# A two-layer graph kernel on one core: two splits moved among earlier units, one convolution kept back for the last batch, the verdict's product moved to the end

## The chip, the cores and the metric

The kernel runs on one core of one Trainium2 chip. The metric is the device time of one execution in microseconds (us); the kernel before takes 3221.36 us, the median of three executions (3220.45 to 3222.96). One core has five engines that run side by side and wait for each other through semaphores: TensorE (PE in the profile: matrix products, with PEld for its weight loads), VectorE (DVE), ScalarE (ACT), GpSimd (POOL) and SyncE (SP, which issues the transfers). Each engine has a queue of its own and works through it in program order.

## What is computed

The input `x` is 32 batches of 512 rows and 512 columns; `adj` is a 512 x 512 matrix of zeros and ones. There are two layers, each with a residual and a layer normalisation. The first is attention with 8 heads of 64 columns, restricted by `adj`; the second multiplies by `adj` from the left and by a weight from the right. Cut to what matters:

```python
def _L0_gnn_ref(x, adj, Wq, bq, Wk, bk, Wv, bv):
    q = (x @ Wq + bq).reshape(b, n, H, HD)          # k and v likewise
    scores = jnp.einsum('bihd,bjhd->bhij', q, k) / jnp.sqrt(jnp.float32(HD))
    scores = scores + jnp.where(adj == 0, -1e9, 0.0)[None, None, :, :]
    weights = jax.nn.softmax(scores, axis=-1)
    return jnp.einsum('bhij,bjhd->bihd', weights, v).reshape(b, n, H * HD)

def _L1_gnn_ref(x, adj, weight, bias):
    y = jnp.einsum('nm,bmd->bnd', adj, x)           # the aggregation
    return jnp.einsum('bnd,do->bno', y, weight) + bias   # the convolution

x = _layernorm(x + _L0_gnn_ref(x, adj, Wq, bq, Wk, bk, Wv, bv), axis=-1)
x = _layernorm(x + _L1_gnn_ref(x, adj, weight, bias), axis=-1)
```

All of it is float32. The kernel computes the first layer's softmax without subtracting a maximum, and ends in a verdict: if the sums of exponentials or the adjacency are out of the expected range, a general kernel computes everything again. With these inputs it isn't run.

## The kernel before

The kernel is scheduled by hand: the order in which the operations are written is the order in each engine's queue. The main loop goes through 32 batches `b` with 4 pairs of heads `hp` each. In every step it writes the scores of the next pair, the attention product of this pair, and then some filler for TensorE, taken from a list of units that belongs to the batch: the projections of batch b + 1 (7 products of a Strassen-Winograd scheme for each of q, k and v, so 21 units), the first layer's normalisation, the aggregation and the convolution of batch b - 1, and the transposes of x of batch b + 2. Each unit has a weight (a convolution unit 1.0, a projection 0.5, an aggregation product 0.55, a transpose unit 0.13, all else 0), and `work_until` takes units until the share of the pair is used up.

TensorE's products go to three PSUM tiles, named `bank`, in rotation; scores have two tiles `ps`, the attention product one, `po`.

```python
    def scores(b, hp, half):
        for j in (2 * half, 2 * half + 1):
            ps = psum.tile([P, 2, N], FP, name="ps", bufs=2)
            for s in range(2):
                ...
                nc.tensor.matmul(ps[:, s, :], keys[:, j * P:(j + 1) * P], queries, start=True, stop=True)
            e = E[b, hp, j] = work.tile([P, 2, N], FP, name="e", bufs=6)
            nc.scalar.activation(e, ps, AF.Exp, scale=1.0 / root)
            nc.vector.tensor_mul(e, e, edge[:, j, None, :].to_broadcast([P, 2, N]))   # the mask, L461
            if j == 1:
                ES[b, hp] = work.tile([P, 2, N], FP, name="es", bufs=3)
                nc.gpsimd.tensor_add(ES[b, hp], E[b, hp, 0], e)
            elif j > 1:
                nc.gpsimd.tensor_add(ES[b, hp], ES[b, hp], e)

    def project(b, which, i):       # one of seven products for q, k or v
        ...
        pm = bank(2, half)
        for r in range(2):
            for d in range(2):
                nc.tensor.matmul(pm[:, r, :], left[:, d, r * P:(r + 1) * P], right[:, d, :], ...)   # L338
        ...                         # then its eviction: on ScalarE for two units of q and k, else on VectorE

    def normalise(t, slot):
        row = X[t - slot // NB][:, slot % NB, :]
        nc.vector.tensor_scalar(row, row, STAT[t][:, slot, 0:1], RSTD[t][:, slot:slot + 1],
                                op0=ALU.subtract, op1=ALU.mult)

    def split(b, d):
        high = HIGH[b, d] = work.tile([P, NB, P], FR, name="high")
        low = LOW[b, d] = work.tile([P, NB, P], FR, name="low")
        cols = X[b][:, :, d * P:(d + 1) * P]
        nc.scalar.activation(high, cols, AF.Copy)
        nc.vector.tensor_sub(low, cols, high.bitcast(FP))

    def aggregate(b, d):
        if d == 0:
            YT[b] = work.tile([P, DB, N], FP, name="yT", bufs=1)
        pm = bank(N)
        parts = [part[:, m, :] for part in (LOW.pop((b, d)), HIGH.pop((b, d))) for m in range(NB)]
        for n, part in enumerate(parts):
            nc.tensor.matmul(pm, part, adjT[:, n % NB, :], start=(n == 0), stop=(n == 2 * NB - 1))
        nc.scalar.activation(YT[b][:, d, :], pm, AF.Copy)
        if d == DB - 1:
            for c in range(NB):
                nc.gpsimd.tensor_add(X[b][:, c, :], X[b][:, c, :], b1_r)

    def convolve(b, c):
        pm = bank(D)
        for d in range(DB):
            nc.tensor.matmul(pm, YT[b][:, d, c * P:(c + 1) * P], w1[:, d, :],
                             start=(d == 0), stop=(d == DB - 1))
        nc.vector.tensor_add(X[b][:, c, :], pm, X[b][:, c, :])
        statistics(b, 1, c)

    def aggregation(b):

        if b < 0:
            return []
        splits, products = ([(f, b, d) for d in range(DB)] for f in (split, aggregate))
        units = splits[:2]
        for d in range(DB):
            units += products[d:d + 1] + splits[d + 2:d + 3]
        return units

    def convolution(b):
        return [(convolve, b, c) for c in range(NB)] if b >= 0 else []
```

[...] ScalarE rounds 128 columns of x to `high`, VectorE subtracts to get `low`, and the aggregation multiplies both by the adjacency, `low` first. `high` and `low` have two buffers each.

The list of a batch's units, and the end of the kernel:

```python
            chores += [(normalise, b - 1, c) for c in range(NB)]
            chores = [(square_root, b - 1, slots), (invert_root, b - 1, slots)] + chores if b > 0 else []
            units = []
            for k, unit in enumerate(made[:-2]):
                units.append((unit, 0.5))
                if k > 0:
                    units += [(u, 0.0) for u in chores[:1]]
                    chores = chores[1:]
            units += [(u, 0.0) for u in chores]
            units += [(u, 0.55 if u[0] is aggregate else 0.0) for u in gathered[:5]]
            units += [(u, 0.5) for u in made[-2:]]
            for unit in gathered[5:]:
                units += [(u, 0.13) for u in turned[:1]] + [(unit, 0.55 if unit[0] is aggregate else 0.0)]
                turned = turned[1:]
            units += [(u, 0.13) for u in turned]
            if b < B - 1:
                units += [(u, 1.0) for u in convolved]
            begun = 0 if b < B - 1 else 1
            share = sum(w for _, w in units) / (HP - 2 * begun)
            done = 0.0
...
        def work_until(part):

            nonlocal done
            begin = share * (hp - begun) + (0.25 if hp % 2 else 0.0)
            end = share * (hp - begun + 1) + (0.0 if hp % 2 else 0.25)
            while units and (units[0][1] == 0 or done < begin + (end - begin) * part - 0.3):
                unit, w = units.pop(0)
                run([unit])
                done += w
...
    run([u for u, _ in units])
    t = B - 1
    rest, gather = convolution(t - 1), aggregation(t)
    run(rest[:2])
    invert(t, 1)
    residual(t, 2)
    residual(t, 3)
    square_root(t, slice(0, NB))
    invert_root(t, slice(0, NB))
    for c in range(NB):
        normalise(t, c)
    run(gather[:2] + rest[2:] + gather[2:])
    if t > 0:
        square_root(t, slice(NB, 2 * NB))
        invert_root(t, slice(NB, 2 * NB))
        for slot in range(NB, 2 * NB):
            normalise(t, slot)
        store(t - 1)
    judge()
    for c in range(NB):
        convolve(t, c)
        slot = NB + c
        square_root(t + 1, slice(slot, slot + 1))
        invert_root(t + 1, slice(slot, slot + 1))
        normalise(t + 1, slot)
        store(t, [c])
```

The list's order in a middle batch is thus: 19 projections, with the normalisations between them; split 0, split 1, product 0, split 2, product 1; the last 2 projections; a transpose unit, split 3, a transpose unit, product 2, a transpose unit, product 3, the last transpose unit; 4 convolution units. `judge()` makes the verdict's 128 flags with seven small VectorE operations, sums them with a one-column matmul, and compares the sum.

Of the kernel before, what the change touches and what calls it, by code (L numbers as in the profile page):

```python
# [39 lines left out]
ALU = mybir.AluOpType  # L40
# [4 lines left out]
P = 128  # L45
# [157 lines left out]
def fast_kernel(ctx: ExitStack, tc, verdict, x, adj, Wq, bq, Wk, bk, Wv, bv, W1, b1, out):  # L203
    nc = tc.nc
    B, N, D = x.shape
    H = Wq.shape[1] // HD
    HP = H // 2
    NB = N // P
    DB = D // P
# [8 lines left out]
    def bank(*shape):  # L218

        return psum.tile([P, *shape], FP, name="bank", tag="bank", bufs=3)  # L220
# [9 lines left out]
    def load_blocks(b):  # L230

        for c in range(NB):
            IN[b, c] = work.tile([P, D], FP, name="xin", bufs=NB)
            nc.sync.dma_start(IN[b, c], x[b, c * P:(c + 1) * P, :])
# [27 lines left out]
    ones = consts.tile([P, P // GROUP], FP, name="ones")  # L262
# [96 lines left out]
    def flips(b):  # L359
        return [(x_transpose, b, c) for c in range(NB)] if b < B else []  # L360

    def projections(b):


        if b >= B:
            return []
        units = [(project, b, which, i) for which in "qkv" for i in ORDER]
        for n in (5, 12):
            units[n:n + 4] = units[n + 2:n + 4] + units[n:n + 2]
        return units  # L370
# [14 lines left out]
    def square_root(t, slots):  # L385
        nc.scalar.activation(RSTD[t][:, slots], STAT[t][:, slots, 1], AF.Sqrt, bias=eps)  # L386

    def invert_root(t, slots):
        nc.vector.reciprocal(RSTD[t][:, slots], RSTD[t][:, slots])  # L389
# [5 lines that stand above are left out]
# [8 lines left out]
    def store(b, blocks=None):  # L403
        for c in blocks or ():
            nc.sync.dma_start(out[b, c * P:(c + 1) * P, :], X[b][:, c, :])
        if blocks is None:
            nc.sync.dma_start(out[b].rearrange("(c p) d -> p c d", p=P), X[b])
# [27 lines left out]

    def aggregation(b):

        if b < 0:
            return []
        splits, products = ([(f, b, d) for d in range(DB)] for f in (split, aggregate))  # L440
        units = splits[:2]
        for d in range(DB):
            units += products[d:d + 1] + splits[d + 2:d + 3]
        return units

    def convolution(b):
        return [(convolve, b, c) for c in range(NB)] if b >= 0 else []
# [4 lines left out]
# [4 lines that stand above are left out]
                lanes = slice(s * HD, (s + 1) * HD)  # L456
                keys, queries = KT[b][hp // 2][lanes, hp % 2, :], QT[b][hp // 2][lanes, hp % 2, :]
# [3 lines that stand above are left out]
            nc.vector.tensor_mul(e, e, edge[:, j, None, :].to_broadcast([P, 2, N]))  # L461
# [5 lines that stand above are left out]
# [52 lines left out]
    def judge():  # L519
        seen = consts.tile([P, 3], FP, name="seen")  # L520
        nc.vector.tensor_reduce(seen[:, 0:1], sums, axis=AX.X, op=ALU.add)
        nc.vector.tensor_reduce(seen[:, 1:2], inverses, axis=AX.XY, op=ALU.add)
        nc.vector.tensor_reduce(seen[:, 2:3], inexact, axis=AX.X, op=ALU.add)
        well = consts.tile([P, 3], FP, name="well")
        nc.vector.tensor_scalar(well[:, 0:2], seen[:, 0:2], BOUND, None, op0=ALU.is_le)
        nc.vector.tensor_scalar(well[:, 2:3], seen[:, 2:3], 0.0, None, op0=ALU.is_equal)
        nc.vector.tensor_mul(well[:, 0:1], well[:, 0:1], well[:, 1:2])
        nc.vector.tensor_mul(well[:, 0:1], well[:, 0:1], well[:, 2:3])
        pm = bank(N)
        nc.tensor.matmul(pm[0:1, 0:1], well[:, 0:1], ones[:, 0:1], start=True, stop=True)  # L530
        nc.vector.tensor_scalar(verdict, pm[0:1, 0:1], P - 0.5, None, op0=ALU.is_lt)


    def run(units):
        for unit in units:
            unit[0](*unit[1:])
# [3 lines left out]
    first = projections(0)  # L540
# [6 lines left out]
    combine(wv, bv_r)  # L547
    run(first[13:])

    pairs = [(b, hp) for b in range(B) for hp in range(HP)]  # L550
    scores(*pairs[0], 0)
    run(flips(1))
    scores(*pairs[0], 1)
    for i, (b, hp) in enumerate(pairs):
        if hp == 0:



            made, turned = projections(b + 1), flips(b + 2)
            gathered, convolved = aggregation(b - 1), convolution(b - 1)  # L560

            slots = slice(0, 2 * NB if b > 1 else NB)
            chores = [(normalise, b - 1, c) for c in [*range(NB, 2 * NB)] * (b > 1)] + [(turn_over, b)] * (b > 1)
            chores += [(normalise, b - 1, c) for c in range(NB)]
            chores = [(square_root, b - 1, slots), (invert_root, b - 1, slots)] + chores if b > 0 else []
            units = []
            for k, unit in enumerate(made[:-2]):
                units.append((unit, 0.5))
                if k > 0:
                    units += [(u, 0.0) for u in chores[:1]]  # L570
                    chores = chores[1:]
            units += [(u, 0.0) for u in chores]
            units += [(u, 0.55 if u[0] is aggregate else 0.0) for u in gathered[:5]]
            units += [(u, 0.5) for u in made[-2:]]
            for unit in gathered[5:]:
                units += [(u, 0.13) for u in turned[:1]] + [(unit, 0.55 if unit[0] is aggregate else 0.0)]
                turned = turned[1:]
            units += [(u, 0.13) for u in turned]
            if b < B - 1:
                units += [(u, 1.0) for u in convolved]  # L580
            begun = 0 if b < B - 1 else 1
            share = sum(w for _, w in units) / (HP - 2 * begun)
            done = 0.0
        if hp == 1 and b + 2 < B:
            load_blocks(b + 2)

        def work_until(part):

            nonlocal done
            begin = share * (hp - begun) + (0.25 if hp % 2 else 0.0)  # L590
            end = share * (hp - begun + 1) + (0.0 if hp % 2 else 0.25)
            while units and (units[0][1] == 0 or done < begin + (end - begin) * part - 0.3):
                unit, w = units.pop(0)
                run([unit])
                done += w

        after = pairs[i + 1] if i + 1 < len(pairs) else None
        if after:
            scores(*after, 0)
        attend(b, hp)  # L600
        if hp % 2:
            add_up(b, hp // 2)
        if after:
            scores(*after, 1)
        else:
            break
        if hp % 2:
            work_until(0.35)
            invert(b, hp // 2)
            work_until(0.6)  # L610
            residual(b, hp - 1)
            residual(b, hp)
        work_until(1.0)
        if hp == HP - 1:
            run([u for u, _ in units])
    run([u for u, _ in units])
    t = B - 1
    rest, gather = convolution(t - 1), aggregation(t)
    run(rest[:2])
    invert(t, 1)  # L620
    residual(t, 2)
    residual(t, 3)
    square_root(t, slice(0, NB))
    invert_root(t, slice(0, NB))
    for c in range(NB):
        normalise(t, c)
    run(gather[:2] + rest[2:] + gather[2:])
    if t > 0:
        square_root(t, slice(NB, 2 * NB))
        invert_root(t, slice(NB, 2 * NB))  # L630
        for slot in range(NB, 2 * NB):
            normalise(t, slot)
        store(t - 1)
    judge()
    for c in range(NB):
        convolve(t, c)
        slot = NB + c
        square_root(t + 1, slice(slot, slot + 1))
        invert_root(t + 1, slice(slot, slot + 1))
        normalise(t + 1, slot)  # L640
        store(t, [c])


# [22 lines left out]
```

## Time and profile before

| | before |
|---|---|
| time, median of 3 | 3221.36 us |
| span in the profile | 3220.5 us |
| granted TensorE clock, mean | 0.994 of full speed |
| a middle batch | about 99 us |
| TensorE's waits for `low` (first operand of an aggregation) | 79.7 us |
| read from and written to the main memory | 33 GB/s |

"Busy" in the profile is time in which an engine executes; the rest is waiting. A timeline is in order of time: start and length in us, the engine, the line of the source, the operation, out<-in, the shapes, how many instructions are merged, and in brackets the idle time before them with what ended it. A float32 matmul is recorded in two passes, so four matmuls of one unit show as x8. How the transfers stand is seen in the page's second part, its slices of 80 us:

```profile
DMA  4001110011110111100111001111011110011000
GB/s 137 14 1 40 40 40 23 18 40 40 40 39 1 40 40 40 39 4 36 40 40 40 23 17 40 40 39 40 1 40 40 40 40 7 33 40 40 27 26 27
```

The first row is the mean busy share of the 16 transfer engines in tenths.

### The profile page before, as it was taken

To read this page: it belongs to the slowest core of one execution; us is meant where nothing else is said; L and a number is where in the kernel's file an instruction comes from. 1 tells how busy PE (TensorE), PEld (TensorE's weight loads), DVE (VectorE), ACT (ScalarE), POOL (GpSimd) and SP (SyncE) were. 2 spreads that over 40 slices of the span, in tenths; PEclk is the share of its full clock that TensorE was granted. 3 is DMA by queue.
4 is the path that set the end of the run, shared out by engine and by line. 5 is a ranking of instruction groups with operands and counts; after the bars stand their busy time and mean duration, and the time that the engine had idled before them with its cause. 6 is when DMAs were issued, how large, how long until landed. Compare 5 with 4: busy or idle time off the path is not lost. (4 is left out here: it accounts for less than half of the span.)

```text
span 3220.5 us, 34020 instructions
## 1 busy us (share of the span) xinstructions
PE 3086.8 (96%) x13330; PEld 1853.7 (58%) x13330; DVE 2009.4 (62%) x2540; ACT 1027.2 (32%) x1509; POOL 1603.7 (50%) x873
## 2 busy tenths in 40 slices
PE   8999999999999999999999999999999999999987
PEld 6656565566555565555656556655556555565643
DVE  6656665656656566665676565665656666566665
ACT  2333233333332333333323323333233333332331
POOL 4645544554455544554554455445554454455442
PEclk9999999999999999999999999999999999999998
DMA  4001110011110111100111001111011110011000
GB/s 137 14 1 40 40 40 23 18 40 40 40 39 1 40 40 40 39 4 36 40 40 40 23 17 40 40 39 40 1 40 40 40 40 7 33 40 40 27 26 27
DMA packets 58005, 108.68 MB, mean 34 GB/s; under 512 B 4336, under 2 KB 7408, under 8 KB 57840
## 3 DMA queue, kind: packets, MB, share of 16 engines
q1 hardware_dynamic: 57840, 106.45, 9.3%
q8 instruction: 107, 1.75, 0.2%
q14 instruction: 58, 0.48, 0.0%
HBM read 72.88 MB, written 33.55 MB: 33 GB/s over the span
## 5 line engine op out<-in xcount | busy, mean ns | idle before, releaser
L461 DVE TENSOR_TENSOR e<-e,edge 128x1024 f32<-128x1024 f32 x512 | 669.8, 1350 | 554.9 <-ACT e L460 554.9
L466 POOL TENSOR_TENSOR es<-es,e 128x1024 f32<-128x1024 f32 x256 | 724.3, 2829 | 260.1 <-DVE e L461 249.9
L464 POOL TENSOR_TENSOR es<-e 128x1024 f32<-128x1024 f32 x128 | 303.2, 2369 | 1089.7 <-DVE e L461 1077.5
L460 ACT ACTIVATE e<-ps 128x1024 f32<-128x1024 f32 x512 | 496.5, 1021 | 1080.8 <-PE ps L458 1080.4
L458 PE MATMUL ps<-q,k 64*128 64x512 f32 x2048 | 511.7, 618 | 6.0 <-ACT e L460 6.0
L475 PE MATMUL po<-e,v 128*64 128x512 f32 x2048 | 467.7, 598 | 0.0
L431 PE MATMUL bank<-w,yT 128*128 128x512 f32 x1024 | 461.1, 599 | 0.4 <-DVE inverse L501 0.4
L338 PE MATMUL bank<-wv,xT 128*128 128x256 f32 x1792 | 421.8, 384 | 20.6 <-DVE k L357 14.0
L338 PE MATMUL bank<-xT,wk 128*128 128x256 f32 x1792 | 410.1, 383 | 2.6 <-PE bank L279 0.9
L338 PE MATMUL bank<-xT,wq 128*128 128x256 f32 x1792 | 401.2, 381 | 2.7 <-DMA wq<-in_L_gnn_Wq_dram 1.4
L338 PEld LDWEIGHTS bank<-wv,xT 128*128 128x128 f32 x1792 | 332.5, 190 | 106.1 <-issue 26.4
L338 PEld LDWEIGHTS bank<-xT,wq 128*128 128x128 f32 x1792 | 337.6, 190 | 71.6 <-DVE e L461 22.0
L338 PEld LDWEIGHTS bank<-xT,wk 128*128 128x128 f32 x1792 | 334.9, 190 | 75.0 <-issue 24.3
L458 PEld LDWEIGHTS ps<-q,k 64*128 64x128 f32 x2048 | 176.9, 187 | 290.6 <-issue 229.1
L475 PEld LDWEIGHTS po<-e,v 128*64 128x64 f32 x2048 | 135.6, 136 | 315.9 <-issue 314.6
L431 PEld LDWEIGHTS bank<-w,yT 128*128 128x128 f32 x1024 | 188.2, 191 | 210.9 <-issue 202.6
L393 DVE TENSOR_SCALAR xs<-xs,stat,rstd 128x512 f32<-128x512 f32 x256 | 297.2, 1183 | 0.3
L426 POOL TENSOR_TENSOR xs<-xs,b_r 128x512 f32<-128x512 f32 x128 | 159.6, 1281 | 176.2 <-DVE low L401 176.2
L422 PE MATMUL bank<-adjT,low 128*128 128x512 f32 x512 | 154.5, 424 | 82.2 <-DVE low L401 79.7
L401 DVE TENSOR_TENSOR low<-xs,high 128x512 fp32r<-128x512 f32 x128 | 179.1, 1419 | 47.6 <-ACT high L400 47.6
L433 DVE TENSOR_TENSOR xs<-bank,xs 128x512 f32<-128x512 f32 x128 | 88.0, 687 | 170.2 <-PE bank L431 153.7
L382 DVE BATCH_NORM_STATS2 bnst<-xs 128x6 f32<-128x512 f32 x256 | 174.6, 682 | 5.5
(89 smaller groups left out, 2398.0 us busy)
## 6 DMA issues: line engine op xcount, KB each, us to landing
xin<-in_x_dram SPq DMA_DIRECT2D x128, 256.0 KB, 5.8
xs<-in_x_dram SPq DMA_DIRECT2D x32, 1024.0 KB, 5.4
out_dram<-xs SPq DMA_DIRECT2D x31, 1024.0 KB, 4.3
wq<-in_L_gnn_Wq_dram SPq DMA_DIRECT2D x2, 512.0 KB, 6.6
wk<-in_L_gnn_Wk_dram SPq DMA_DIRECT2D x2, 512.0 KB, 8.5
yT<-in_adj_dram SPq DMA_DIRECT2D x1, 1024.0 KB, 7.6
wv<-in_L_gnn_Wv_dram SPq DMA_DIRECT2D x2, 512.0 KB, 8.4
w<-in_L_gnn_weight_dram SPq DMA_DIRECT2D x1, 1024.0 KB, 11.8
```

The source lines that it names most:

```text
L338: nc.tensor.matmul(pm[:, r, :], left[:, d, r * P:(r + 1) * P], right[:, d, :], start=(d == 0), stop=(d == 1))
L382: nc.vector.bn_stats(st, X[b][:, c, :])
L393: nc.vector.tensor_scalar(row, row, STAT[t][:, slot, 0:1], RSTD[t][:, slot:slot + 1], op0=ALU.subtract, op1=ALU.mult)
L401: nc.vector.tensor_sub(low, cols, high.bitcast(FP))
L426: nc.gpsimd.tensor_add(X[b][:, c, :], X[b][:, c, :], b1_r)
L431: nc.tensor.matmul(pm, YT[b][:, d, c * P:(c + 1) * P], w1[:, d, :], start=(d == 0), stop=(d == DB - 1))
L458: nc.tensor.matmul(ps[:, s, :], keys[:, j * P:(j + 1) * P], queries, start=True, stop=True)
L460: nc.scalar.activation(e, ps, AF.Exp, scale=1.0 / root)
L461: nc.vector.tensor_mul(e, e, edge[:, j, None, :].to_broadcast([P, 2, N]))
L464: nc.gpsimd.tensor_add(ES[b, hp], E[b, hp, 0], e)
L466: nc.gpsimd.tensor_add(ES[b, hp], ES[b, hp], e)
L475: nc.tensor.matmul(po[s * HD:(s + 1) * HD, :], values, e[:, s, :], start=(j == 0), stop=(j == NB - 1))
```

## The change

The change reorders work and leaves the computation as it is. It has three parts.

- **Two splits earlier.** In the batches 1 to 30 the first two splits of the aggregation no longer stand directly ahead of the first product, but behind projections 14 and 15 of 19 (counted from 0), which fall among the units of the second pair of heads. The third split stays behind the first product; the fourth comes after the first transpose unit. The transposes shift a little: units 0 and 1 stand ahead of products 2 and 3, the other two at the end.
- **One convolution kept back.** Batch 30 no longer runs the convolution of batch 29. The last batch, which has no projections and transposes to fill TensorE with, runs it during its first pair, together with the first layer's normalisation of batch 30 and its first two splits; the second layer's normalisation of batch 29 follows there.
- **The verdict's product at the end.** The flags are made ahead of the last convolution unit; the matmul that sums them, and the comparison, are the last operations.

The aim is that VectorE and ScalarE have their results ready when TensorE comes to need them, and that TensorE has work where others are still busy. The core of the diff (cuts marked "..."):

```diff
     def aggregation(b):
-        if b < 0:
-            return []
-        splits, products = ([(f, b, d) for d in range(DB)] for f in (split, aggregate))
-        units = splits[:2]
-        for d in range(DB):
-            units += products[d:d + 1] + splits[d + 2:d + 3]
-        return units
+        return [[(f, b, d) for d in range(DB)] if b >= 0 else [] for f in (split, aggregate)]
...
     # in judge()
-        pm = bank(N)
-        nc.tensor.matmul(pm[0:1, 0:1], well[:, 0:1], ones[:, 0:1], start=True, stop=True)
-        nc.vector.tensor_scalar(verdict, pm[0:1, 0:1], P - 0.5, None, op0=ALU.is_lt)
+        return well[:, 0:1]
...
+    def units_of(b):
+        made, turned = projections(b + 1), flips(b + 2)
+        splits, gathered = aggregation(b - 1)
+        young, old = norm(b - 1, 0), norm(b - 1, 1)
+        ready = [(turn_over, b)] if b > 1 else []
+        if b == B - 1:
+            older = convolution(b - 2)
+            units = young[:2] + older[:1] + young[2:4] + older[1:2] + young[4:] + older[2:3] + splits[:1]
+            units += older[3:] + splits[1:2] + old + ready
+            first = sum(w for _, w in weighed(units))
+            for d in range(DB):
+                units += gathered[d:d + 1] + splits[d + 2:d + 3]
+            return weighed(units), [first, first + 1.1, first + 2.2, first + 2.2]
+        if old:
+            old[:2] = [(f, b - 1, slice(0, 2 * NB)) for f in (square_root, invert_root)]
+            young = young[2:]
+        chores = old + ready + young
+        units, made, late = [], made[:-2], made[-2:]
+        early = len(made) - 5
+        for k, unit in enumerate(made):
+            units.append(unit)
+            if k > 0:
+                units += chores[:1]
+                chores = chores[1:]
+            if 0 <= k - early < 2:
+                units += splits[k - early:k - early + 1]
+        units += gathered[:1] + splits[2:3] + gathered[1:2] + late + turned[:1] + splits[3:]
+        units += gathered[2:3] + turned[1:2] + gathered[3:] + turned[2:]
+        if b < B - 2:
+            units += convolution(b - 1)
+        units = weighed(units)
+        whole = sum(w for _, w in units)
+        return units, [whole / HP * (hp + 1) + (0.0 if hp % 2 else 0.25) for hp in range(HP)]
...
-            work_until(0.6)
+            work_until(0.6 if b < B - 1 else 1.0)
             residual(b, hp - 1)
             residual(b, hp)
...
-    judge()
     for c in range(NB):
+        if c == NB - 1:
+            well = judge()
         convolve(t, c)
         slot = NB + c
         square_root(t + 1, slice(slot, slot + 1))
         invert_root(t + 1, slice(slot, slot + 1))
         normalise(t + 1, slot)
         store(t, [c])
+    pm = bank(N)
+    nc.tensor.matmul(pm[0:1, 0:1], well, ones[:, 0:1], start=True, stop=True)
+    nc.vector.tensor_scalar(verdict, pm[0:1, 0:1], P - 0.5, None, op0=ALU.is_lt)
```

## The prediction, made before the changed kernel ran

> **What bounds the kernel now.** I read the page's first part, then TensorE's waits, then the timelines of one middle batch (about 99 us of the span) and of the end. The page's busy times:

> ```profile
> PE 3086.8 (96%) x13330; PEld 1853.7 (58%) x13330; DVE 2009.4 (62%) x2540; ACT 1027.2 (32%) x1509; POOL 1603.7 (50%) x873
> ```

> TensorE is the bound; the other engines have a third of their time or more to spare. Since all instructions stay, only time in which TensorE waits, or runs at a lower clock, can be won. The view of waits, TensorE's alone (receiver, producer, then total us, times, longest):

> ```profile
> PE bank L422 <- DVE low L401: 79.7, 60, 3.1
> PE bank L338 <- DVE k L357: 14.0, 28, 0.5
> PE ps L458 <- ACT e L460: 6.0, 3, 5.4
> PE bank L530 <- DVE well L528: 5.0, 1, 5.0
> ```

> The first line is the aggregation's product waiting for the low half of a split: 60 waits, two in nearly every batch. The same view cut to 97 to 3010 us has 74.0 us in 57 waits, none over 1.8 us, so these belong to the steady part, batches 1 to 29. TensorE's timeline of a middle batch shows both:

> ```profile
> 1582.13 3.72 PE L338 MATMUL bank<-wv,xT 128*128 128x256 f32 x16
> 1587.68 1.19 PE L422 MATMUL bank<-adjT,low 128*128 128x512 f32 x4 [1.82 <-DVE low L401]
> 1588.71 1.09 PE L422 MATMUL bank<-adjT,high 128*128 128x512 f32 x4
> 1590.58 1.17 PE L422 MATMUL bank<-adjT,low 128*128 128x512 f32 x4 [0.78 <-DVE low L401]
> 1591.59 1.09 PE L422 MATMUL bank<-adjT,high 128*128 128x512 f32 x4
> 1592.51 3.61 PE L338 MATMUL bank<-wv,xT 128*128 128x256 f32 x16
> ```

> Two projections, then the first two aggregations, each preceded by idle time (in brackets), 2.60 us together. VectorE's timeline tells why:

> ```profile
> 1582.51 2.36 DVE L461 TENSOR_TENSOR e<-e,edge 128x1024 f32<-128x1024 f32 x2 [3.14 <-ACT e L460]
> 1584.79 0.68 DVE L352 TENSOR_TENSOR v<-bank,v 128x512 f32<-128x512 f32 x1
> 1585.89 0.69 DVE L357 TENSOR_TENSOR v<-bank,v 128x512 f32<-128x512 f32 x1 [0.42 <-PE bank L338]
> 1586.50 3.93 DVE L401 TENSOR_TENSOR low<-xs,high 128x512 fp32r<-128x512 f32 x2
> ```

> The split's subtractions stand in VectorE's queue behind the eviction of the projection that TensorE has only just finished. They cannot start until TensorE is about to want them, and then take 1.96 us each. The end of the run:

> ```profile
> 3132.73 3.79 PE L458 MATMUL ps<-q,k 64*128 64x512 f32 x8 [5.39 <-ACT e L460]
> ...
> 3196.23 0.19 PE L530 MATMUL bank<-ones,well 128*1 128x1 f32 x2 [5.03 <-DVE well L528]
> 3196.35 16.79 PE L431 MATMUL bank<-w,yT 128*128 128x512 f32 x32
> ```

> Two long waits, and after each the matmuls are slow: 3.79 us for eight score matmuls that take 1.99 elsewhere, 16.79 us for 32 convolution matmuls of which 16 take 7.03 elsewhere.

> [...] the subtractions wait behind an eviction on which they don't depend. [...] the granted clock is 0.57 between 3196 and 3203 us, after the wait of 5.03 us, while waits of 1.82 us leave it at 1.00. [...] the two subtractions took 3.93 us beside GpSimd's additions of 1583.88 to 1589.89, and the batch's last took 0.69 at 1597.75 with GpSimd idle. [...] here the bubble ends with new data, so another buffer would not help.

> **The change part by part.**

> 1. *First two splits among the second pair's units (batches 1 to 30).* By the weights, the second pair takes the projections up to number 16 (counted from 0), and the splits now follow 14 and 15. On VectorE the order becomes k, low, k, low, v, then the masks of the next scores. In the trace these evictions start at 1571.86, 1573.16 and 1574.82, with 0.62, 0.97 and 1.49 us idle ahead of the second, third and the masks. GpSimd is idle from 1568.63 to 1579.52, so I take 0.69 us for a subtraction, not 1.96. The chain: k to 1572.5, low to 1573.2, k to 1573.9, low to 1574.6, v at 1574.8 as before. ScalarE's two copies (0.6 us each) fall into its idle stretch of 16.5 us. The rows are ready too: the last normalisation ends at 1567.3. So nothing is delayed, and both halves lie ready some 11 us before the first product. Gain: 74.0 us in batches 1 to 29.

> 2. *The later splits.* The third split still comes after the first product; two projections (3.6 us) and four transposes pass before its product, so it stays hidden. The fourth is tighter. It starts after the first transposes are copied, 0.6 us after they end, needs 0.6 us on ScalarE and 0.69 on VectorE (GpSimd is done by then), thus 2.0 us. TensorE meanwhile has one product (2.0) and four transposes (0.4), thus 2.4 us. 0.4 us is spare: I book no wait, but it is the thinnest spot.

> 3. *Batch 30.* It loses its two waits (1.82 + 0.76) and, through the convolution kept back, 14 us of TensorE work that goes to batch 31, so pairs follow each other sooner. In the second pair VectorE then has about 18 us of work (masks 4.7, evictions 4 to 5, normalisations 6, residuals 2.8) to TensorE's 21, with banks held meanwhile. I allow 2 us of new waits there in place of the 0.65 of now: a net gain of 1.2 us.

> 4. *Batch 31, first pair.* Now it has no filler: the next scores follow at once, and VectorE runs eight normalisations (7.57 us) ahead of the splits, with the next exponentials behind those on ScalarE. The kept-back convolution gives TensorE 14 us in that spot, and half of the normalisations stand between its evictions. Waits there now: 0.33 (scores), 2.06 (sum of exponentials), 5.39 (scores), 2.47 and 0.43 (aggregation and convolution behind the inverse), 10.7 us. The low clock costs another 1.8 + 1.0 us (scores at 3.79 and 2.98 instead of 1.99) + 0.6 (high products at 1.69 instead of 1.09), 3.4. I allow 2 us for new waits, since ScalarE's table load (1.28) and a square root still stand before the third pair's exponentials. Gain: 12.1 us.

> 5. *Verdict's product at the very end.* The last convolution no longer stands behind the verdict's matmul, which waited for four normalisations and seven small operations. It can start when the last aggregation is copied: that product ends at 3191.20, the copy at 3191.84, so 0.64 us stay of 5.03 and 4.4 go. With a gap that short the clock holds: 16.79 − 2 × 7.03 = 2.7 us more. Against it, judging moves ahead of the last block's eviction (0.9 us in VectorE's gap of 0.69, so 0.2) and the verdict follows the last normalisation (0.15). Gain: 6.8 us.

> The final wait of 3.1 us for a low half, behind the last residuals and normalisations, has the same order before and after and stays. Sum: 74.0 + 1.2 + 12.1 + 6.8 = 94.1 us; 3221.4 − 94.1 = **3127 us**, 2.9% less.

> **The rivals.** *A wait that takes the place of the one removed.* If the fourth split's margin of 0.4 us is not there, its product waits, at most about 0.9 us if its subtraction runs at 1.96 us. Over 29 batches that gives back up to 26 us: 3153. For it speaks how thin the margin is; against it, that GpSimd was idle when this subtraction ran. *VectorE becomes the bound of the second pair.* It has idle time there, but TensorE already waits 0.5 us for k's eviction in 28 batches. If the added copies and subtractions fall beside GpSimd's work, they cost 2.6 us more and push v's eviction and the masks; attention needs those masks only a pair later, so perhaps 0.5 us a batch returns: 3141. *The bubble was slack for others.* If ScalarE, VectorE or GpSimd set the batch's pace, TensorE would only wait elsewhere and little would be gained: 3200. Against it: 62% on the busiest of them, and no wait for scores in the steady part. *The other way,* if the 0.5 us waits go too: 14 us more, 3113.

> **Range and chances.** Parts 1 and 5 are read straight off the trace; parts 3 and 4 are allowances, 5 us either way; the fourth split could cost 10 to 26 us. Hence 3113 to 3143, longer above. A gain of 2% needs 64.4 us: the steady part alone gives it, and only the whole of the first rival with failing ends, or the third rival, takes it away: 94% faster, 5% within 2%, 1% slower.

> **What would show it right or wrong.** Right: TensorE's wait for low falls from 79.7 us in 60 waits to a handful, about 3 us long in all; the first two subtractions take about 0.69 us; a middle batch lasts 2.6 us less; the wait for the verdict is gone and the last 32 convolution matmuls take about 14 us. Step 2 is wrong if waits for low remain, about 30, ahead of the fourth product; step 1, if waits for k or v grow, or subtractions of about 2 us stand between those evictions; steps 3 and 4, if waits in the last 200 us stay above 12 us. The number as a whole is wrong if TensorE's idle time only changes its name.

## The result, and the profile after

The changed kernel takes 3104.4 us (median of four, 3102.95 to 3105.36) against 3222.2 us (four executions) for the one before: a ratio of 0.9634, with a 95% interval of 0.9618 to 0.9651. That is 117.8 us less. The prediction had 94.1 us, 3127 us, and a range that began at 3113: the direction was right, the gain a fifth too small.

The first part of the page shows something that the prediction did not count on:

```profile
PE 3059.6 (99%) x13330; PEld 1856.9 (60%) x13330; DVE 1941.1 (63%) x2541; ACT 1030.7 (33%) x1510; POOL 1585.1 (51%) x873
```

TensorE runs as many instructions as before, 13330, yet its busy time has fallen by 27.2 us (from 3086.8), 23.6 of them in the batches 1 to 28. The prediction is 23.7 us short: a hint where to look. TensorE's waits (receiver, producer, total us, times, longest) look as predicted:

```profile
PE bank L338 <- DVE k L357: 14.0, 28, 0.5
PE bank L307 <- DMA xin<-in_x_dram: 4.1, 2, 3.6
PE bank L422 <- DVE low L401: 3.1, 1, 3.1
...
PE bank L653 <- DVE well L522: 0.3, 1, 0.3
```

Of 60 waits for `low` one is left, that of the end; the waits for k stay at 14.0 us; the verdict's wait fell from 5.0 to 0.3 us and has nothing behind it. VectorE's timeline of a middle batch has the subtractions in their new place, 0.68 us each where they took 1.96:

```profile
1526.79 0.68 DVE L357 TENSOR_TENSOR k<-bank,k 128x512 f32<-128x512 f32 x1
1527.38 0.68 DVE L401 TENSOR_TENSOR low<-xs,high 128x512 fp32r<-128x512 f32 x1
1528.09 0.69 DVE L357 TENSOR_TENSOR k<-bank,k 128x512 f32<-128x512 f32 x1
1528.70 0.68 DVE L401 TENSOR_TENSOR low<-xs,high 128x512 fp32r<-128x512 f32 x1
```

And TensorE's timeline of the same batch, from the last two projections to the next two:

```profile
1537.06 3.72 PE L338 MATMUL bank<-wv,xT 128*128 128x256 f32 x16
1540.43 1.28 PE L422 MATMUL bank<-adjT,low 128*128 128x512 f32 x4
1541.55 1.10 PE L422 MATMUL bank<-adjT,high 128*128 128x512 f32 x4
1542.49 1.09 PE L422 MATMUL bank<-adjT,low 128*128 128x512 f32 x4
1543.42 1.09 PE L422 MATMUL bank<-adjT,high 128*128 128x512 f32 x4
1544.35 3.61 PE L338 MATMUL bank<-wv,xT 128*128 128x256 f32 x16
```

Here lies the surplus. Read the first column only. From the projections' start to the first product it was 5.55 us before (1582.13 to 1587.68) and is 3.37 now: 2.18 us less, though the idle time in brackets was 1.82. The reason is in the second column: the projections are recorded as 3.72 us long, but the product begins 3.37 us after their start. The recorded end of the last of them lies 0.35 us beyond the point where the product can start. A gap counted from that end is short by that much. From the first to the second product: 2.90 before, 2.06 now, 0.84 less with 0.78 shown. From there to the projections: 1.93 and 1.86. In sum 3.09 us a batch, where the waits show 2.60.

A middle batch, measured from one sum of exponentials to the same one a batch later (median of batches 1 to 28), fell from 99.04 to 95.70 us, by 3.34. The other 0.25 is a second wait that the waits never showed; the experiments name it.

The end of the run, TensorE again:

```profile
3004.60 14.00 PE L431 MATMUL bank<-w,yT 128*128 128x512 f32 x32
...
3025.02 1.99 PE L452 MATMUL ps<-q,k 64*128 64x512 f32 x8
...
3081.04 13.89 PE L431 MATMUL bank<-w,yT 128*128 128x512 f32 x32
3095.20 0.19 PE L653 MATMUL bank<-ones,well 128*1 128x1 f32 x2 [0.27 <-DVE well L522]
```

The convolution kept back fills the last batch's first pair, the third pair's scores run at full clock (1.99 us at a granted clock of 1.00, not 3.79 at 0.50), and so does the last convolution (13.89 us at 1.00, not 16.79 at 0.83).

### The profile page after: what moved, and what is told of

It reads as the page before. It is cut to its first block, busy times and chain, and to the rows that moved or that the text cites. A ratio compares the mean times of both kernels' runs of the same rounds, so it can differ in the third digit from the quotient of the medians.

```text
span 3103.6 us, 33940 instructions
## 1 busy us (share of the span) xinstructions
PE 3059.6 (99%) x13330; PEld 1856.9 (60%) x13330; DVE 1941.1 (63%) x2541; ACT 1030.7 (33%) x1510; POOL 1585.1 (51%) x873
## 4 chain that ended last, share of the span: by engine, by line
PE 89%; DVE 7%; issue 2%; ACT 1%; SPq 0%; POOL 0%; DMA 0%; ACTq 0%; DVEq 0%; POOLq 0%
PE bank L338 31%; PE ps L452 15%; PE po L469 15%; PE bank L431 14%; PE bank L422 8%; DVE e L455 2%; PE bank L480 2%; DVE xs L393 2%; PE bank L307 2%; PE bank L502 2%; ACT e L454 1%; DVE k L352 1%; DVE k L357 1%; DVE k L350 1%; PE bank L493 0%
## 5 line engine op out<-in xcount | busy, mean ns | idle before, releaser
L455 DVE TENSOR_TENSOR e<-e,edge 128x1024 f32<-128x1024 f32 x512 | 679.4, 1368 | 585.9 <-ACT e L454 585.8
L458 POOL TENSOR_TENSOR es<-e 128x1024 f32<-128x1024 f32 x128 | 302.3, 2362 | 1078.4 <-DVE e L455 1065.8
L460 POOL TENSOR_TENSOR es<-es,e 128x1024 f32<-128x1024 f32 x256 | 716.3, 2798 | 249.4 <-DVE e L455 239.3
L431 PE MATMUL bank<-w,yT 128*128 128x512 f32 x1024 | 457.8, 595 | 0.4 <-DVE inverse L495 0.4
L338 PE MATMUL bank<-wv,xT 128*128 128x256 f32 x1792 | 424.2, 386 | 20.0 <-DVE k L357 14.0
L338 PE MATMUL bank<-xT,wk 128*128 128x256 f32 x1792 | 410.3, 383 | 3.1 <-PE bank L279 0.9
L338 PE MATMUL bank<-xT,wq 128*128 128x256 f32 x1792 | 401.3, 381 | 2.5 <-DVE wq L295 1.4
L338 PEld LDWEIGHTS bank<-wv,xT 128*128 128x128 f32 x1792 | 334.3, 191 | 105.3 <-issue 26.4
L338 PEld LDWEIGHTS bank<-xT,wq 128*128 128x128 f32 x1792 | 337.5, 190 | 72.3 <-DVE e L455 22.0
L338 PEld LDWEIGHTS bank<-xT,wk 128*128 128x128 f32 x1792 | 334.9, 190 | 75.3 <-issue 23.5
L431 PEld LDWEIGHTS bank<-w,yT 128*128 128x128 f32 x1024 | 187.4, 190 | 210.1 <-issue 202.5
L401 DVE TENSOR_TENSOR low<-xs,high 128x512 fp32r<-128x512 f32 x128 | 110.6, 865 | 97.0 <-ACT high L400 97.0
L472 ACT ACTIVATE attT<-po 128x512 f32<-128x512 f32 x128 | 76.4, 597 | 277.7 <-PE po L469 277.7
## 6 DMA issues: line engine op xcount, KB each, us to landing
w<-in_L_gnn_weight_dram SPq DMA_DIRECT2D x1, 1024.0 KB, 10.5
```

## The experiments

Three theories for the surplus were set against each other. **A:** a wait costs the distance between the starts of the matmuls around it, which is more than the idle time shown. **B:** the steady part brought what was shown, and the two ends brought more. **C:** VectorE's shorter subtractions gave relief. Times are medians of four; the kernel before took 3222 us beside each of them.

**e1, the splits alone.** The kernel before, with this edit (and the list cut accordingly):

```diff
+                if gathered and k in (14, 15):
+                    units.append((gathered[0], 0.0))
+                    gathered = gathered[1:]
```

> The kernel before with its first two splits moved behind projections 14 and 15 and nothing else changed (transposes and both ends as before). Theory A, a wait of TensorE costs the distance between the starts of the matmuls around it, which is 0.35 and 0.16 us more than the idle time shown, since the end of a matmul lies beyond the start of the next: a middle batch falls from 99.03 us by 2.60 + 0.5 to about 95.95, the time by some 92 us to 3130 (3126 to 3134). Theory B, only the idle time shown is won in the steady part and the surplus of 23 us over the prediction comes from the two ends: 3145. Theory C, the surplus comes from VectorE's 68 us of shorter subtractions and the transposes' new places: between the two, with a middle batch at 96.4.

Measured: 3128.8 us (ratio 0.9710, 0.9694 to 0.9726), a middle batch of 95.93 us. Theory A had 3130 and 95.95. The splits alone bring 93.4 us, nearly the whole of the prediction's sum, where 74 to 77 were booked. Theory B is out. The middle batch also decides against C's 96.4. The single starts decide it more sharply. Cut a middle batch into TensorE's 39 stretches of one kind of operation, each lasting until the next begins. From the kernel before to e1, the stretches around products 0 and 1 are 3.09 us shorter; each of the others agrees within 0.02 us. VectorE's shorter subtractions brought nothing anywhere else.

**e2, the transposes in their old places.**

```diff
-        units += gathered[2:3] + turned[1:2] + gathered[3:] + turned[2:]
+        units += turned[1:2] + gathered[2:3] + turned[2:3] + gathered[3:] + turned[3:]
```

> The changed kernel with the transposes back in their old places (units 0 and 1 on either side of nothing but the fourth split, ahead of product 2, unit 2 ahead of product 3). Theory A: product 2 then takes the bank of the second late projection, whose eviction ends 0.7 us after the projection's last matmul, and its first matmul starts 0.25 us after the last transpose instead of 0.03; no idle time is recorded, as the transposes' recorded ends cover it. A middle batch lasts 0.24 us more, the time 7 us more: 3111 (3109 to 3113), with no new line in TensorE's waits. The rival, that the order of transposes does nothing: 3104.

Measured: 3110.0 us, 5.6 more than the changed kernel; a middle batch 95.93 us, 0.24 more. The waits of the steady part have no new line. TensorE's timeline of this kernel:

```profile
1549.91 1.04 PE L307 MATMUL bank<-ident,xin 128*128 128x128 f32 x8
1550.91 1.20 PE L422 MATMUL bank<-adjT,low 128*128 128x512 f32 x4
```

And of the changed kernel, with four records of transposes ahead of the product instead of eight:

```profile
1547.80 0.60 PE L307 MATMUL bank<-ident,xin 128*128 128x128 f32 x4
1548.15 1.18 PE L422 MATMUL bank<-adjT,low 128*128 128x512 f32 x4
```

No bracket in either, and the transposes seem to run into the product. In the single records the product starts 0.24 us after the last transpose's start in e2, and 0.03 us after it in the changed kernel. With two transposes ahead of it, product 2 takes the bank of the second late projection, whose eviction has just ended; with one, it takes a bank that came free a unit earlier. That the three banks in rotation set this is read from the order of the tiles; the cost of 0.24 us is measured.

**e3, the verdict's product as before.** The lines of `judge()` and the product go back ahead of the last convolution.

> The changed kernel with the verdict's product ahead of the last convolution, as before. As predicted in step 5, 6.8 us are lost: 3111 (3109.5 to 3113), a wait of 5 us for the flags and 16 to 17 us for the last 32 convolution matmuls. If the two ends hold the surplus (theory B), more: 3115 or above.

Measured: 3110.3 us, 5.9 more. The wait of 5.0 us and the 16.66 us of the last 32 convolution matmuls are back, as predicted.

**e4, nothing kept back.**

```diff
-            older = convolution(b - 2)
+            older = []
...
-        if b < B - 2:
+        if b < B - 1:
             units += convolution(b - 1)
```

> The changed kernel with the convolution of batch 29 run in batch 30 as before, so that the last batch's first pair has no filler again. As predicted in steps 3 and 4: 13.3 us lost, 3118 (3113 to 3122), and waits of 8 to 11 us in all for exponentials, sums and inverses in the last batch, with the clock below full. If the two ends hold the surplus (theory B): 3125 or above.

Measured: 3111.9 us, 7.5 more, below the expected range. TensorE's timeline of the last batch in this kernel:

```profile
3026.83 1.14 PE L480 MATMUL bank<-es,ones 128*32 128x512 f32 x4 [2.06 <-POOL es L460]
3031.78 3.78 PE L452 MATMUL ps<-q,k 64*128 64x512 f32 x8 [3.81 <-ACT e L454]
```

The waits are back, but not all: 3.81 us instead of 5.39, and 0.54 instead of 2.47 for the inverse. The reason is a part of the change that the prediction booked under the convolution: in the last batch the younger normalisations and the splits now stand ahead of the older normalisations, and e4 leaves that order in. By difference it is worth about 5 us: from batch 29's first sum of exponentials to the end, e1 takes 272.6 us and e4 262.1; of these 10.5 us, 5.3 belong to the verdict (258.9 in e3 against 253.6) and about 0.5 to the transposes of two batches. No run has this order alone.

**e5, one split late.** A dose of the wait, put back in:

```diff
-            if 0 <= k - early < 2:
-                units += splits[k - early:k - early + 1]
-        units += gathered[:1] + splits[2:3] + ...
+            if k - early == 1:
+                units += splits[1:2]
+        units += splits[:1] + gathered[:1] + splits[2:3] + ...
```

> The changed kernel with split 0 alone put back directly ahead of product 0 (split 1 stays behind projection 15). Its subtraction again stands behind the eviction of projection 18 and beside GpSimd's additions, so product 0 should show an idle time of about 1.82 us as before. Theory A (a wait costs start to start, here 2.20 us from the last projection matmul to the first product matmul, against 0.03 without a wait, less 0.08 in the matmul after it): a middle batch of 97.8 us, the time 3166 (3162 to 3170). If a wait cost only the idle time shown: 97.5 us and 3158. If only VectorE's relief counted (theory C: one subtraction of about 1.3 us more): 96.4 us and 3125.

Measured: the median middle batch is 97.80 us, theory A's number to the digit, with an idle time of 1.82 us shown each time. But the kernel takes 3189.7 us (3182.6 to 3192.5), 24 us more than expected, and A does not say why. In the profiled execution, of 3182.6 us, 12 of 28 middle batches last 99.3 us or more. The windows of two batches around the wait, with the granted clock as the third column from the end, tell (columns: window, its length, busy time and instructions of PE, PEld, DVE, ACT, POOL, then clock, DMA share, GB/s):

```profile
1578.00:1581.00 3.00, 2.33 (x10) 1.93 (x11) 0.61 (x1) 0.17 (x1) 2.92 (x3) 1.00 0.00 0
1581.00:1585.00 4.00, 4.00 (x20) 3.40 (x19) 1.20 (x2) 1.54 (x3) 2.72 (x2) 1.00 0.00 0
1676.00:1679.00 3.00, 2.54 (x9) 2.05 (x10) 0.41 (x1) 0.00 (x0) 3.00 (x2) 0.82 0.00 0
1679.00:1683.00 4.00, 4.00 (x15) 3.26 (x14) 1.55 (x1) 1.71 (x3) 2.17 (x2) 0.71 0.00 0
```

In the first batch the clock stays at 1.00; in the second it is at half for 3.41 us, and 15 matmuls run in the time of 20. The clock falls to half behind the same wait of 1.82 us in 12 batches and not in the others. The 28 batches last 17.5 us longer in all than 28 times the median, about 1.5 us for each of the 12, which is what this execution has over the expected 3166. The other three executions took 6 to 10 us longer, with a mean granted clock of 0.988 to 0.990 where this one has 0.992. The last section looks at these waits again.

**e6, the normalisations sooner.** The 28 waits for k that the change left:

```diff
-                units += chores[:1]
-                chores = chores[1:]
+                few = 2 if k > 3 else 1
+                units += chores[:few]
+                chores = chores[few:]
```

> The changed kernel with two chores (normalisations) per projection from unit 4 on, so that all are done in the first pair's units and none stands between the evictions of the second pair. The 28 waits for k, 14.0 us in all, should go. Theory A: each costs 0.66 us start to start and 0.10 in the next matmul, thus 0.77 a batch, and the unit before it shows another 0.2 to 0.3 of unrecorded waiting: 21 to 29 us, 3076 to 3083, a middle batch of about 94.8. If only the idle time counted: 3090. Rival: the first pair then has too much for VectorE, and a wait of a few tenths for q appears there: 3090 to 3105.

Measured: 3076.7 us (ratio 0.9547, 0.9531 to 0.9563), 27.7 less than the changed kernel. The waits for k, 14.0 us by the idle time, were worth twice that: a middle batch fell by 1.03 us to 94.67, with 0.50 us shown. TensorE's timelines of the two projections, the changed kernel first and e6 below:

```profile
1518.99 1.99 PE L338 MATMUL bank<-wv,xT 128*128 128x256 f32 x8
1521.48 1.99 PE L338 MATMUL bank<-wv,xT 128*128 128x256 f32 x8 [0.50 <-DVE k L357]
...
1505.43 3.62 PE L338 MATMUL bank<-wv,xT 128*128 128x256 f32 x16
```

From the start of the first to the transposes behind the second it is 0.87 us less; another 0.17 went ahead of the first, where no bracket stood. No wait for q took their place in the steady part; batch 30 got one of 2.5 us.

**e7, the splits behind projections 11 and 12.**

```diff
-        early = len(made) - 5
+        early = len(made) - 8
```

> The changed kernel with the first two splits behind projections 11 and 12 in place of 14 and 15: still in the second pair and long ahead of their products, but beside GpSimd's additions and the normalisations. If only being early mattered: 3104. If the place counts because VectorE is the bound of this stretch (the prediction's second rival): subtractions of 1.2 to 2 us, the waits for k grow from 0.5 to about 2 or 3 us a batch, the time to 3150 (3130 to 3175). No wait for low in either case.

Measured: 3148.0 us, 43.6 more, and no wait for `low`. So the place counts, as the prediction's second rival said. But the subtractions are not slow there: in a middle batch they take 0.98 and 0.67 us. VectorE's line of the first, then TensorE's timeline:

```profile
1540.95 0.98 DVE L401 TENSOR_TENSOR low<-xs,high 128x512 fp32r<-128x512 f32 x1 [0.70 <-ACT high L400]
...
1539.50 2.00 PE L338 MATMUL bank<-wv,xT 128*128 128x256 f32 x8 [0.50 <-DVE k L357]
1542.16 1.20 PE L502 MATMUL bank<-ident,attT 128*128 128x128 f32 x8 [0.67 <-DVE inverse L495]
1543.90 3.72 PE L338 MATMUL bank<-xT,wk 128*128 128x256 f32 x16 [0.54 <-DVE v L344]
```

The wait for k is what it was. Two new ones follow it, since the subtraction stands in VectorE's queue ahead of the inverse and of v's eviction, and had itself to wait 0.70 us for ScalarE's copy of rows just normalised.

**e8 and e9, a version that beats both.** e8 is e6 with one convolution unit instead of two ahead of the last residuals (`rest[:1]` and `rest[1:]`); e9 keeps one chore per projection in batch 30.

> As e6, and at the end one convolution unit instead of two ahead of the last residuals, so that three follow them while VectorE does the last statistics, normalisations and subtractions. The last wait of 3.1 us should fall below 1 us and the clock hold: 4 us less than e6 (2.5 to 5). If the eviction of those three units holds the products up instead: no gain.

> As e8, but batch 30, which has fewer projections in its first pair, keeps one chore per projection; in e8 it shows a wait of 2.5 us for the eviction of q ahead of the residuals. That wait should fall to the 0.5 us of the changed kernel: 1.5 to 2.5 us less than e8, about 3071. It is meant as the version that beats both kernels.

Measured: 3073.2 and 3070.3 us. In e8 the wait of 3.1 us has fallen to 0.6, with a new one of 0.8 us for an eviction beside it, and the time by 3.5 us; e9 gains another 2.9, a little more than expected. e9 stands at 0.9528 (0.9512 to 0.9544) of the kernel before, 34 us below the changed kernel.

**e10, a small dose.**

```diff
-            if 0 <= k - early < 2:
-                units += splits[k - early:k - early + 1]
-        units += gathered[:1] + ...
+            if k == early:
+                units += splits[:1]
+        units += splits[1:2] + gathered[:1] + ...
```

> The changed kernel with split 1 alone put back ahead of product 0 (split 0 stays early): a smaller dose of the wait of e5. Its subtraction starts behind the eviction of projection 18 and ends 1.2 to 2.0 us later, product 1 would start 1.0 us after that eviction: a delay of 0.3 to 1.0 us a batch, of which up to 0.2 us is covered by recorded ends and not shown as idle. Theory A: a middle batch at 96.0 to 96.7 us, the time 3113 to 3134, longer than the idle time shown accounts for. And with so short a wait the granted clock should stay full in every middle batch, while in e5 it fell to half for 3.4 us in 12 of them (1.5 us each): if those dips come from the length of the wait and not from there being a wait, none here.

Measured: 3114.0 us, 9.6 more than the changed kernel; a middle batch 96.03 us, 0.33 more. TensorE's timeline:

```profile
1545.28 1.28 PE L422 MATMUL bank<-adjT,low 128*128 128x512 f32 x4
1546.39 1.09 PE L422 MATMUL bank<-adjT,high 128*128 128x512 f32 x4
1547.58 1.17 PE L422 MATMUL bank<-adjT,low 128*128 128x512 f32 x4
```

From one product to the next it is 2.30 us instead of 2.06 (the rest of the 0.33 lies in the matmuls just behind), and no bracket shows it: the gap to the recorded end is 0.09 us, too little for the view. The waits list no line for `low` but that of the end. Nearly 10 us are lost to a wait that can be found only by comparing starts. The mean granted clock is 0.998 in all four executions, as in the changed kernel (0.997 to 0.998), and full in all middle batches: a wait this short brought none of the falls that 1.82 us brought in 12 batches of e5.

## Why the prediction was wrong

- **Step 1** is the step that failed, by the size of one term. It said "Gain: 74.0 us in batches 1 to 29": the idle time of the waits, added up. These batches brought 98 us. The mechanism was right in each point: the waits for `low` went from 60 to one, the subtractions took 0.68 us, nothing was delayed, the waits for k stayed. But the cost of a wait is the distance between starts. It is 2.18 and 0.84 us where 1.82 and 0.78 are shown, and 0.07 in the matmuls behind. 0.49 us a batch over 29 batches makes 14 us. e1, e5 and e10 show it from three sides: taken away, put back large, put back small.
- The same step took no account of the transposes' shift. It removed an unshown wait for a bank of 0.24 us a batch, 7 us (e2: 5.6 in the times, 6.6 in the 28 batches of the trace).
- **Step 2** held: no wait ahead of the fourth product.
- **Steps 3 and 4**, 13.3 us together, were near as a sum, which is about 15, and not in their reason. Keeping the convolution back is worth 7.5 us (e4); 3.1 us are batch 30's own two splits (91.87 us from its first sum of exponentials to that of batch 31 before, 88.77 in e1); about 5 us, by difference, are the new order of the last batch's normalisations and splits.
- **Step 5**: 6.8 us predicted, 5.9 measured (e3).
- **The range** was too narrow at its lower end. "The other way" took the 0.5 us waits as its only reserve. They stayed, and the time was below 3113 all the same. They would have been worth 27.7 us, not 14 (e6).
- The first rival (a wait at the fourth product) and the third (another engine sets the pace) did not come. The second came in part for a place three projections earlier (e7): v's eviction was pushed back, but the subtractions were not slow.

The sum closes: the middle batches brought 98 us (95.0 in 28 of them, 3.3 in the next) instead of 74, of which 1.4 us are two batches of before that ran at half clock for a while. From batch 30 on it was 22 instead of 20, and the first 170 us of this profile took 3 us longer than those of before, with the waits for the first transfers differing and two stretches of 3.41 us at half clock, at 42.11 and 137.68 us, where the profile of before has none. That gives 117.

## What to carry to other kernels

Count a wait of TensorE from start to start, against the same pair of instructions where it runs without a wait; the idle time shown leaves out the length by which a recorded end overhangs the next start (0.35 us behind the projections here), and short waits vanish altogether (the 0.24 us in e2 and in e10). A sign of it here was that the busy time fell by 27.2 us though no instruction went: a recorded end that runs into a wait counts as busy. And an operation moved ahead in an engine's queue must be put where its inputs are ready and nothing urgent stands behind it: here, three projections earlier cost 44 us.

## What the runs showed of the hardware

A wait of 1.82 us was followed in some batches by 3.41 us at half of TensorE's clock, and in others not. In the steady part of the kernel before there are 29 waits for `low` of 1.82 or 1.83 us. Behind 27 of them the granted clock is 1.00; behind two, which began at 1188.24 and 1288.17 us, it is 0.50 for 3.41 us (the prediction, which has the clock at 1.00 after waits of 1.82 us, missed these two). In e5 it was 12 of 28 batches. So a wait of the same length cost 2.2 us or 3.7 us.

The shorter wait of the kernel before, 0.75 to 0.78 us in 26 batches, was never followed by half clock, although 10 of them began between 0.03 and 0.17 of a step. From which length on a wait halves the clock stays open between 0.78 and 1.82 us.
